# Group statistics of the first layer's output: sums from ScalarE's accumulator output in place of VectorE's bn_stats

## The chip, the cores and the metric

The kernel runs on one core of one Trainium2 chip. The metric is the device time of an execution in microseconds (us), the median of several runs. In what follows PE is the tensor engine (PEld its weight loads), DVE the vector engine, ACT the scalar engine, POOL GpSimd, and SP the engine whose queue issues most of the DMAs.

## The reference

The input `x` is (4, 16, 256, 256) in float32: four images, 16 channels. Two layers follow each other, each with a residual connection:

```python
x = x + _L0_conv_ref(_gn(x), L0_conv_conv_w, L0_conv_conv_b)
x = x + _L1_conv_ref(_gn(x), L1_conv_base_weight, ..., L1_conv_bias_weight)
```

`_gn` normalises each image in 8 groups of two channels: it subtracts the group's mean and divides by sqrt(var + 1e-5), over all 256 x 256 pixels. Layer 0 is a convolution that gives 25 logits for each channel and pixel, a softmax over the 25, and a sum of the 5 x 5 neighbourhood of the normalised `x` weighted by it. Layer 1 is a convolution of SiLU and of eight B-spline bases of its normalised input. What this document is about lies between the two: layer 1's normalisation needs the mean and the variance of each group of layer 0's output `x1`, and an image's statistics are known only once its last pixel is there.

## The kernel before

**Preparation** (to about 142 us). The statistics of `x` are taken with `bn_stats` on DVE, put together over the partitions by a matmul with a matrix of ones (`group_stats`, L132 to L153), and kept for each image as `nrm[b]`: column 0 is the reciprocal standard deviation of each group, column 1 is minus mean times that. So `x * nrm[:, 0] + nrm[:, 1]` is the normalised `x`. Image 0 is normalised here.

**Layer 0** (about 142 to 2110 us) goes over 64 strips: 4 images, 2 halves of 128 rows (the rows lie on the partitions), 8 strips of 32 columns. A strip is eight iterations of four columns. In each iteration:

- PE makes the logits, two columns to a tile `lg`, of which there are three (L775 and L779, two matmuls a column).
- ACT takes their exponential into a tile `e`, of which there are four (two ACTIVATEs of 800 elements, L798).
- POOL multiplies `e` with the neighbourhood `u` into the second half of `e` (L803).
- DVE sums numerator and denominator over the 25 places, for the iteration before (L680). This frees the `e` buffer for the exponential four iterations on.

After a strip's last sums, DVE and ACT make the quotient: `Ln` and `Exp` on ACT (L693, L694), three operations on DVE (L698 to L700), in `seed` and `divide`. POOL subtracts the result from the tile `xc` (`apply`, L706; the signs are such that this adds the layer's output to `x`). `xc` holds 128 columns, so four strips. After the fourth it holds `x1`; its statistics are taken (`statistics`, L711, eight `bn_stats` of 256 elements on DVE, L714) and it is stored to `x1s` by a DMA that ACT issues (`store`, L724).

What is done when is written out by hand: `after(k, f)` puts `f` on a list, and `step()` at the end of each iteration calls what is due. So `f` is emitted behind the work of the (k+1)-th iteration after this one. Each engine works through its instructions in the order in which they were emitted (`in_order`, L571). After the last strip the list is emptied without iterations between.

While an image runs, the next one is normalised (`normalize`, L238) by a generator that is advanced once an iteration: on ACT the normalised rows `hsp` and `ht` (L312, L325) and copies `tt` and `hi` out of PSUM (L340), on PE transposes, on DVE the difference `lo` (L355). For image 3 there is nothing more to normalise. In its place the scales of layer 1 for images 0 and 1 are worked out there (`scales`, L166, advanced twice a strip); those of images 2 and 3 follow in layer 1. `scales` turns the statistics into `q`, whose columns are the scale and the bias with which layer 1 reads `x1`.

**Layer 1** (about 2119 us to the end) has 64 units of 16 rows. Per unit ACT does for each of two halves an `Abs` (L923) and three functions (L158, L159, L160 in `spline`), and one `Silu` (L908). DVE does four operations a half (L161 to L164) and moves the result out of PSUM (L944). PE does 120 matmuls. The instructions of layer 1 that need no more than layer 0's early rows are emitted into the last strips of layer 0: `marks` says behind which instruction of ACT's and SP's queue they may begin. The first `Silu` stands behind the last ACT instruction of layer 0.

Of the kernel before, what the change touches and what calls it, by code (L numbers as in the profile page):

```python
# [11 lines left out]
F32 = mybir.dt.float32  # L12
F32R = mybir.dt.float32r
AF = mybir.ActivationFunctionType
ALU = mybir.AluOpType
AX = mybir.AxisListType
# [17 lines left out]
def conv_preact_kernel(  # L34
# [12 lines left out]
    nc = tc.nc  # L47
    B, C, H, W = x.shape
    G = 8
    GC = C // G  # L50
# [77 lines left out]

    edge = const.tile([P, 5], F32, name="edge")
    stat1 = ctx.enter_context(tc.tile_pool(name="stat1", bufs=1))  # L130
    st1 = [const.tile([P, G, NH * (W // CX), 6], F32, name=f"st1_{b}") for b in range(B)]

    def group_stats(pool, psum, st, name):

# [31 lines left out]
    def scales(b, psum):  # L166


        def small(n, name):
            return stat1.tile([P, n], F32, name=f"{name}_{b}", tag=f"{name}{b % 2}")  # L170

        mv = stat1.tile([P, G, 2], F32, name=f"mv_{b}", tag=f"mv{b % 2}")
        for g in range(G):
            nc.vector.bn_aggr(mv[:, g, :], st1[b][:, g].rearrange("p n s -> p (n s)"))
        yield
        ps = psum()[:, 0:G]
        nc.tensor.matmul(ps, lhsT=ones, rhs=mv[:, :, 0], start=True, stop=True)
        yield
        mean, d, rstd = small(G, "mean"), small(G, "d"), small(G, "rstd")
        q = stat1.tile([P, 6], F32, name=f"q_{b}", tag=f"q{b}")  # L180
        nc.vector.tensor_sub(d, mv[:, :, 0], ps)
        nc.vector.tensor_mul(mean, gsel_sb, ps)
        nc.vector.reduce_sum(q[:, 1:2], mean, AX.X)
        yield
        nc.scalar.activation(d, d, AF.Square)
        yield
        ps = psum()[:, 0:G]
        nc.tensor.matmul(ps, lhsT=ones, rhs=d, start=True, stop=False)
        nc.tensor.matmul(ps, lhsT=ones, rhs=mv[:, :, 1], start=False, stop=True)
        yield  # L190
        nc.vector.tensor_scalar(rstd, ps, EPS, None, ALU.add)  # L191
        yield
        nc.gpsimd.tensor_tensor(rstd, rstd, mhalf, ALU.pow)  # L193
        nc.gpsimd.tensor_mul(rstd, rstd, gsel_sb)
        yield
        nc.vector.reduce_sum(q[:, 0:1], rstd, AX.X)
        nc.vector.tensor_scalar(q[:, 1:2], q[:, 1:2], q[:, 0:1], -1.0, ALU.mult, ALU.mult)
        for k in range(2):
            nc.vector.tensor_scalar(q[:, 2 + k : 3 + k], q[:, k : k + 1], 2.5, None, ALU.mult)
        yield  # L200
        ps = psum()[:, 0:2]
        nc.tensor.matmul(
            ps, lhsT=sel.rearrange("p c s -> p (c s)"), rhs=q[0:C, 2:4], start=True, stop=True
        )
        yield
        nc.vector.tensor_copy(q[:, 4:5], ps[:, 0:1])
        nc.vector.tensor_add(q[:, 5:6], ps[:, 1:2], ub)
        sc[b] = tuple(q[:, k : k + 1] for k in (0, 1, 4, 5))
        yield
# [2 lines left out]


    nrm = [const.tile([P, 2, G], F32, name=f"nrm{b}") for b in range(B)]
    NIM = 3

    def norm_tiles(prep):
# [171 lines left out]
    with tc.tile_pool(name="prep0", bufs=2) as prep, tc.tile_pool(  # L389
# [121 lines left out]
        for b in range(B):  # L511
            st = stat.tile([P, G, NH * (GC if b == 0 else 1), 6], F32, name=f"st0_{b}", tag=f"st0{min(b, 1)}")
            for hf in range(NH):
                n = b * NH + hf
                t = loaded.pop(0)
                for g in range(G):
                    if b == 0:
                        for k in range(GC):
                            nc.vector.bn_stats(st[:, g, hf * GC + k, :], t[:, g * GC + k, :])
                    else:  # L520
                        nc.vector.bn_stats(
                            st[:, g, hf, :],
                            t[:, g * GC : (g + 1) * GC, :].rearrange("p c w -> p (c w)"),
                        )
                    next(ahead, None)
                    next(ahead, None)

                nc.scalar.activation(xq, t, AF.Square)
                sq = pstat.tile([P, W], F32, name=f"sq_{n}", tag="sq")
                for c in range(C):  # L530
                    nc.tensor.matmul(
                        sq, lhsT=idr, rhs=xq[:, c], start=c == 0, stop=c == C - 1
                    )
                nc.vector.tensor_reduce(hm[:, n : n + 1], sq, AX.X, ALU.max)
                next(ahead, None)
                if n >= NH and n + 3 < B * NH:
                    loaded.append(load_x(n + 3))
            mean, rstd = group_stats(stat, pstat, st, f"x{b}")
            nc.vector.tensor_copy(nrm[b][:, 0], rstd)
            nc.vector.scalar_tensor_tensor(nrm[b][:, 1], mean, -1.0, rstd, ALU.mult, ALU.mult)  # L540
            ms = stat.tile([P, 2], F32, name=f"ms_{b}", tag="ms")
            nc.vector.tensor_mul(mean, mean, mean)
            nc.vector.tensor_reduce(ms[:, 0:1], mean, AX.X, ALU.add)
            nc.vector.tensor_scalar(ms[:, 0:1], ms[:, 0:1], 9.0 * GC, None, ALU.mult)
            nc.vector.tensor_reduce(ms[:, 1:2], rstd, AX.X, ALU.max)
            nc.vector.tensor_mul(ms[:, 1:2], ms[:, 1:2], ms[:, 1:2])
            v = hm[:, b * NH : (b + 1) * NH]
            nc.vector.tensor_scalar(v, v, 9.0 / 8.0, ms[:, 0:1], ALU.mult, ALU.add)
            nc.vector.tensor_scalar(v, v, ms[:, 1:2], None, ALU.mult)
            if b == 0:  # L550
                prepare0()
            if b == 1:
                prepare1()
            if b == 0:
                ahead = normalize(0, ptr0, tiles, held, nc.vector.tensor_copy)
                next(ahead)
# [41 lines left out]
    def layer0(shift):  # L598
# [4 lines left out]
        with tc.tile_pool(name=f"prep{arm}", bufs=2) as prep, tc.tile_pool(  # L603
# [64 lines left out]
            def after(k, f, *args):  # L668

                later.append([k, partial(f, *args)])  # L670
# [32 lines left out]
            def apply(n, nd, xc):  # L703
                w0 = strips[n][2] * SW % CX
                v = xc[:, :, w0 : w0 + SW]
                nc.gpsimd.tensor_sub(v, v, nd[:, 1].rearrange("p j c -> p c j"))  # L706
                if w0 + SW == CX:
                    after(2, statistics, n, xc)

            def statistics(n, xc):  # L710
                b, hf, s = strips[n]  # L711
                k = hf * (W // CX) + s * SW // CX
                for g in range(G):
                    nc.vector.bn_stats(  # L714
                        st1[b][:, g, k, :],
                        xc[:, g * GC : (g + 1) * GC, :].rearrange("p c w -> p (c w)"),
                    )
                after(2, store, n, xc)

            def store(n, xc):  # L720
                b, hf, s = strips[n]
# [104 lines left out]
    def layer1(arm, last, marks):  # L826
# [3 lines left out]
        with ExitStack() as pools:  # L830
# [124 lines left out]
            def outputs(n, sx):  # L955
# [27 lines left out]
                waiting.append((b, u, yp))  # L983

            more = chain(*(
                scales(b, lambda: pstat.tile([P, 8], F32, name=f"ps{arm}", tag="ps"))
                for b in range(2, B)
            ))
            for half in range(2):
# [90 lines left out]
```

## Time and profile before

The time is 3223.17 us, the median of three runs (3222.82 to 3223.66). The page of the profiled execution has a span of 3222.0 us:

| engine | busy us | share of the span | instructions |
|---|---|---|---|
| PE | 2862.3 | 89% | 14776 |
| PEld | 1490.7 | 46% | 14776 |
| DVE | 3101.7 | 96% | 1799 |
| ACT | 2208.0 | 69% | 2233 |
| POOL | 1936.4 | 60% | 659 |

These are averages over two stages with different limits. The tenths of the span in 40 slices tell the stages apart: ACT stands at 4 to 6 tenths and POOL at 9 until the 28th slice, and from there ACT at 9 and POOL at 0. DVE stands at 9 nearly throughout.

In the lists of groups, an instruction is named by its line, engine and operation, then by the tiles it writes and reads. "Idle before" is time in which the engine stood still just before these instructions, with what ended it. In lists in order of time the first number is the start, the second the time from the first start to the last end, and "x8" says that eight instructions follow each other.

### The profile page before, as it was taken

Reading aid. Unit: us, or ns where it says so; the run is one execution under the profiler, and the core shown is the slowest. Engines: PE = TensorE matmul, PEld = TensorE weight load, DVE = VectorE, ACT = ScalarE, POOL = GpSimd, SP = SyncE. Lnnn points to the kernel's source line nnn. Section 1 sums busy time; section 2 is a strip of 40 time slices with the busy share of each in tenths; the row PEclk is TensorE's granted clock in tenths of the full one; section 3 lists DMA queues with packets and bytes.
Section 4 is the critical chain, followed back from the end, with each engine's and each line's share of the span. In section 5 each row is a group of like instructions: output and inputs, shape, how many; then the busy total and the mean of one; then the engine's idle time right before and its main releaser. Section 6 shows DMA issues by size and latency. Waiting matters only on the chain. (4 is left out here: it accounts for less than half of the span.)

```text
span 3222.0 us, 40428 instructions
## 1 busy us (share of the span) xinstructions
PE 2862.3 (89%) x14776; PEld 1490.7 (46%) x14776; DVE 3101.7 (96%) x1799; ACT 2208.0 (69%) x2233; POOL 1936.4 (60%) x659
## 2 busy tenths in 40 slices
PE   3499999999999999999999989859999989988988
PEld 3366665666566566656656656512222222222222
DVE  6589999999999999999999999999999999999997
ACT  6366555466554465554444444589999999999996
POOL 2299999999999999999999999900000000000000
PEclk7699999999999999999999999979999999999999
DMA  7988886778877788877756756678878778888883
GB/s 224 291 223 236 229 221 187 212 211 230 246 208 192 203 219 225 249 198 203 210 156 170 191 157 170 163 169 183 178 168 179 180 171 168 180 176 173 178 179 71
DMA packets 356531, 626.34 MB, mean 194 GB/s; under 512 B 45298, under 2 KB 222692, under 8 KB 340452
## 3 DMA queue, kind: packets, MB, share of 16 engines
q1 hardware_dynamic: 323300, 606.88, 75.3%
q10 hardware_dynamic: 33024, 16.78, 1.9%
q8 instruction: 121, 1.98, 0.3%
q14 instruction: 86, 0.70, 0.1%
HBM read 513.95 MB, written 104.24 MB: 192 GB/s over the span
## 5 line engine op out<-in xcount | busy, mean ns | idle before, releaser
L775 PE MATMUL lg<-wm,am 128*128 128x400 f32 x4096 | 1748.9, 508 | 123.4 <-ACT e L798 109.7
L803 POOL TENSOR_TENSOR e<-e,u 128x1600 f32<-128x1600 f32 x512 | 1789.1, 3536 | 68.5 <-ACT e L798 68.0
L680 DVE TENSOR_REDUCE nd<-e 128x128 f32<-128x3200 f32 x512 | 1747.5, 3477 | 23.3 <-POOL e L803 23.2
L798 ACT ACTIVATE e<-lg 128x800 f32<-128x800 f32 x1024 | 815.7, 836 | 896.5 <-DVE nd L680 768.9
L779 PE MATMUL lg<-wn,an 97*128 97x400 f32 x2048 | 1358.4, 663 | 0.5 <-DMA an<-hsl 0.5
L775 PEld LDWEIGHTS lg<-wm,am 128*128 128x128 f32 x4096 | 766.3, 194 | 450.1 <-ACT e L798 161.3
L961 PE MATMUL yp<-ring,wt 128*32 128x512 f32 x6144 | 755.1, 604 | 146.0 <-DVE ring L164 110.4
L779 PEld LDWEIGHTS lg<-wn,an 97*128 97x128 f32 x2048 | 390.8, 191 | 311.9 <-issue 15.6
L961 PEld LDWEIGHTS yp<-ring,wt 128*32 128x32 f32 x6144 | 206.5, 110 | 685.1 <-issue 477.9
L889 POOL MEMSET sx<- 16x256 f32 x8 | 2.4, 303 | 765.6 <-DMA out_dram<-yo 706.6
L977 PE MATMUL yp<-sl,ws 64*32 64x512 f32 x1536 | 176.5, 588 | 0.0
L164 DVE TENSOR_TENSOR ring<-ta,ta 128x2048 f32<-128x2048 f32 (+1 forms) x64 | 147.8, 2309 | 2.5
L164 DVE TENSOR_TENSOR ring<-tb,tb 128x2048 f32<-128x2048 f32 x64 | 145.6, 2276 | 2.6
L163 DVE TENSOR_TENSOR ta<-ta,ta 128x2048 f32<-128x2048 f32 (+1 forms) x64 | 147.3, 2301 | 0.0
L163 DVE TENSOR_TENSOR tb<-tb,tb 128x2048 f32<-128x2048 f32 x64 | 146.5, 2289 | 0.0
L908 ACT ACTIVATE sl<-sx,q 64x2048 f32<-64x2048 f32 x64 | 133.3, 2083 | 0.0
L160 ACT ACTIVATE ta<-ta 128x2048 f32<-128x2048 f32 (+1 forms) x64 | 122.3, 1911 | 0.0
L160 ACT ACTIVATE tb<-tb 128x2048 f32<-128x2048 f32 x64 | 120.5, 1883 | 0.6 <-POOL sx L889 0.6
L193 POOL TENSOR_TENSOR rstd<-rstd,mhalf 128x8 f32<-128x8 f32 x4 | 8.7, 2176 | 175.6 <-DVE rstd L191 175.6
L706 POOL TENSOR_TENSOR xc<-xc,nd 128x512 f32<-128x512 f32 x64 | 98.8, 1544 | 12.1 <-DVE nd L700 12.1
L977 PEld LDWEIGHTS yp<-sl,ws 64*32 64x32 f32 x1536 | 48.8, 106 | 116.2 <-issue 113.2
L923 ACT ACTIVATE xta<-xta,q 128x2048 f32<-128x2048 f32 (+2 forms) x44 | 91.6, 2083 | 0.0
(174 smaller groups left out, 2131.9 us busy)
## 6 DMA issues: line engine op xcount, KB each, us to landing
am<-hst SPq DMA_DIRECT2D x512, 194.6 KB
u<-hs SPq DMA_DIRECT2D x320, 288.0 KB
an<-hsl SPq DMA_DIRECT2D x512, 129.8 KB
xta<-x1s SPq DMA_DIRECT2D x40, 1024.0 KB
xtb<-x1s SPq DMA_DIRECT2D x40, 1024.0 KB
xtc<-x1s SPq DMA_DIRECT2D x40, 1024.0 KB
am<-hst SPq DMA_DIRECT2D x256, 129.8 KB
sx<-x1s SPq DMA_DIRECT2D x248, 128.0 KB
```

Source lines behind the costliest of these rows:

```text
L160: nc.scalar.activation(s1, r1, AF.Square, scale=2.0)
L163: nc.vector.tensor_mul(s1, s1, r1)
L164: nc.vector.tensor_add(f, s2, s1)
L680: nc.vector.tensor_reduce(nd[:, :, j : j + JG, :], e.rearrange("p t j m c d -> p t j c m d"), AX.XY, ALU.add,)
L706: nc.gpsimd.tensor_sub(v, v, nd[:, 1].rearrange("p j c -> p c j"))
L775: nc.tensor.matmul(lg[:, i, :NL], lhsT=am[:, o : o + P], rhs=wm.rearrange("p m c d -> p (m c d)"), start=True, stop=False,)
L779: nc.tensor.matmul(lg[:, i, :NL], lhsT=an[:, o : o + P], rhs=wn.rearrange("p m c d -> p (m c d)"), start=False, stop=True,)
L798: nc.scalar.activation(ev, lg[:, :, :NL], AF.Exp)
L803: nc.gpsimd.tensor_tensor(e[:, 1].rearrange("p j m c d -> p j (m c) d"), e[:, 0].rearrange("p j m c d -> p j (m c) d"), uv, ALU.mult,)
L908: nc.scalar.activation(sl[n % 2][:, :, 1 : W + 1], t, AF.Silu, scale=sc[b][0][0 : RD * C], bias=sc[b][1][0 : RD * C],)
L961: nc.tensor.matmul(yp[t * M : (t + 1) * M], lhsT=wt[:, d, e].rearrange("p r o -> p (r o)"), rhs=ring[:, r0 + t * RT + d : r0 + t * RT + d ...
L977: nc.tensor.matmul(yp[t * M : (t + 1) * M], lhsT=ws[:, e].rearrange("p r o -> p (r o)"), rhs=sl[n % 2][:, t : t + NT + 1 : NT, e : e + W], ...
```

## The change

`bn_stats` and `bn_aggr` leave layer 1's statistics. In their place each group of `xc` is passed twice over ACT, once as `Identity` and once as `Square`, both with scale `nrm[b][:, 0]` and bias `nrm[b][:, 1]` of the group of `x`. So ACT forms z = (x1 - mean of x) / std of x, and its accumulator output gives the sum of z and of its square over the 256 elements; the written tile `z` itself is read by nobody. The sums of z and of z squared give mean and variance of x1 in units of the group of `x`, which keeps both near the size of one. The purpose is to take the statistics off DVE, which is the busiest engine in layer 0.

The statistics are also spread: one group in each of eight iterations instead of all eight at once, from one iteration earlier on. The store of `xc` is no longer put off behind the statistics and comes three iterations earlier, behind the second group. `scales` is rewritten for the sums: fewer operations on DVE, one matmul instead of three, and five operations on POOL instead of two. It needs `nrz[b]`, two more small operations an image in the preparation.

```diff
--- before
+++ after
@@ -128,7 +128,10 @@
-    st1 = [const.tile([P, G, NH * (W // CX), 6], F32, name=f"st1_{b}") for b in range(B)]
+    NK = NH * W // CX
+    st1 = [const.tile([P, 2, G, NK], F32, name=f"st1_{b}") for b in range(B)]
@@ -169,32 +172,29 @@ scales
-        mv = stat1.tile([P, G, 2], F32, name=f"mv_{b}", tag=f"mv{b % 2}")
-        for g in range(G):
-            nc.vector.bn_aggr(mv[:, g, :], st1[b][:, g].rearrange("p n s -> p (n s)"))
+        sums, d, mz, p = small(2 * G, "sums"), small(G, "d"), small(G, "mz"), small(G, "p")
+        q = stat1.tile([P, 6], F32, name=f"q_{b}", tag=f"q{b}")
+        nc.vector.tensor_reduce(sums, st1[b].rearrange("p t g k -> p (t g) k"), AX.X, ALU.add)
         yield
-        ps = psum()[:, 0:G]
-        nc.tensor.matmul(ps, lhsT=ones, rhs=mv[:, :, 0], start=True, stop=True)
+        ps = psum()[:, 0 : 2 * G]
+        nc.tensor.matmul(ps, lhsT=ones, rhs=sums, start=True, stop=True)
         yield
-        mean, d, rstd = small(G, "mean"), small(G, "d"), small(G, "rstd")
-        q = stat1.tile([P, 6], F32, name=f"q_{b}", tag=f"q{b}")
-        nc.vector.tensor_sub(d, mv[:, :, 0], ps)
-        nc.vector.tensor_mul(mean, gsel_sb, ps)
-        nc.vector.reduce_sum(q[:, 1:2], mean, AX.X)
+        part = 1.0 / (GC * CX * NK)
+        nc.scalar.activation(d, ps[:, 0:G], AF.Square, scale=part)
         yield
-        nc.scalar.activation(d, d, AF.Square)
+
+        nc.vector.scalar_tensor_tensor(mz, ps[:, 0:G], part, nrm[b][:, 1], ALU.mult, ALU.subtract)
+        nc.vector.scalar_tensor_tensor(d, ps[:, G : 2 * G], part, d, ALU.mult, ALU.subtract)
         yield
-        ps = psum()[:, 0:G]
-        nc.tensor.matmul(ps, lhsT=ones, rhs=d, start=True, stop=False)
-        nc.tensor.matmul(ps, lhsT=ones, rhs=mv[:, :, 1], start=False, stop=True)
+        nc.gpsimd.tensor_add(d, d, nrz[b][:, 1])
+        nc.gpsimd.tensor_tensor(p, d, mhalf, ALU.pow)
+        nc.gpsimd.tensor_mul(d, p, nrz[b][:, 0])
+        nc.gpsimd.tensor_mul(p, p, gsel_sb)
+        nc.gpsimd.tensor_mul(p, p, mz)
         yield
-        nc.vector.tensor_scalar(rstd, ps, EPS, None, ALU.add)
-        yield
-        nc.gpsimd.tensor_tensor(rstd, rstd, mhalf, ALU.pow)
-        nc.gpsimd.tensor_mul(rstd, rstd, gsel_sb)
-        yield
-        nc.vector.reduce_sum(q[:, 0:1], rstd, AX.X)
-        nc.vector.tensor_scalar(q[:, 1:2], q[:, 1:2], q[:, 0:1], -1.0, ALU.mult, ALU.mult)
+        nc.vector.reduce_sum(q[:, 0:1], d, AX.X)
+        nc.vector.reduce_sum(q[:, 1:2], p, AX.X)
+        nc.vector.tensor_scalar(q[:, 1:2], q[:, 1:2], -1.0, None, ALU.mult)
...
+    nrz = [const.tile([P, 2, G], F32, name=f"nrz{b}") for b in range(B)]
@@ -538,6 +541,8 @@
             nc.vector.scalar_tensor_tensor(nrm[b][:, 1], mean, -1.0, rstd, ALU.mult, ALU.mult)
+            nc.gpsimd.tensor_mul(nrz[b][:, 0], rstd, gsel_sb)
+            nc.vector.scalar_tensor_tensor(nrz[b][:, 1], rstd, EPS, rstd, ALU.mult, ALU.mult)
@@ -705,17 +710,20 @@ apply, statistics
                 if w0 + SW == CX:
-                    after(2, statistics, n, xc)
-
-            def statistics(n, xc):
+                    for g in range(G):
+                        after(1 + g, statistics, n, xc, g)
+                    after(2, store, n, xc)
+
+            def statistics(n, xc, g):
                 b, hf, s = strips[n]
                 k = hf * (W // CX) + s * SW // CX
-                for g in range(G):
-                    nc.vector.bn_stats(
-                        st1[b][:, g, k, :],
-                        xc[:, g * GC : (g + 1) * GC, :].rearrange("p c w -> p (c w)"),
-                    )
-                after(2, store, n, xc)
+                z = l0.tile([P, GC * CX], F32, name=f"z_{n}_{g}{arm}", tag="z")
+                v = xc[:, g * GC : (g + 1) * GC, :].rearrange("p c w -> p (c w)")
+                for t, f in enumerate((AF.Identity, AF.Square)):
+                    nc.scalar.activation(
+                        z, v, f, scale=nrm[b][:, 0, g : g + 1], bias=nrm[b][:, 1, g : g + 1],
+                        accum_out=st1[b][:, t, g, k : k + 1],
+                    )
```

More of the change, by code (lines that the diff above doesn't have):

```diff
@@ L985, in layer1 @@
             more = chain(*(
-                scales(b, lambda: pstat.tile([P, 8], F32, name=f"ps{arm}", tag="ps"))
+                scales(b, lambda: pstat.tile([P, 2 * G], F32, name=f"ps{arm}", tag="ps"))
                 for b in range(2, B)
```

## The prediction

> **What bounds the kernel now.** I read the busy time by stretch first, then groups, waits, and single engines in order of time. Layer 0 with image 1 to 3's normalisation runs from about 171 to 2110 us, layer 1 from 2119.5 on. The busy time in these stretches (length, then PE, weight loads, DVE, ACT, POOL, each with its count):
>
> ```profile
> 171.00:2110.00 1939.00, 1810.90 (x6297) 1169.58 (x6295) 1928.05 (x906) 1043.87 (x1532) 1872.66 (x577) 0.98 0.75 203
> 2110.00:2119.50 9.50, 0.00 (x0) 0.00 (x0) 9.21 (x12) 3.25 (x4) 1.38 (x9) 0.50 0.85 209
> 2119.50:3222.00 1102.50, 981.77 (x8208) 267.40 (x8208) 1059.40 (x609) 1072.05 (x570) 22.49 (x27) 0.98 0.80 169
> ```
>
> In layer 0 DVE is busy 99.4%, POOL 96.6%, ACT 54%. In layer 1 ACT works without a gap until 3195 us (its waits after 2119.5 are none). So the change takes work from the engine that bounds layer 0 and gives it to the engine that bounds layer 1, but mostly while that one idles. The groups (line, engine, operation, tiles, shapes, count, busy us, mean ns, idle before):
>
> ```profile
> L680 DVE TENSOR_REDUCE nd<-e 128x128 f32<-128x3200 f32 x512 | 1747.5, 3477 | 23.3 <-POOL e L803 23.2
> ...
> L798 ACT ACTIVATE e<-lg 128x800 f32<-128x800 f32 x1024 | 815.7, 836 | 896.5 <-DVE nd L680 768.9 <-PE lg L779 109.7 <-DVE q L196 3.7
> L714 DVE BATCH_NORM_STATS2 st<-xc 128x6 f32<-128x256 f32 x128 | 43.2, 410 | 1.6 <-POOL xc L706 1.6
> ```
>
> ACT's exp waits for DVE's reduce to free one of the four `e` buffers. The other waits of layer 0, in the list of who waited for whom between 171 and 2110 us:
>
> ```profile
> ACT e L798 <- PE lg L779: 95.0, 138, 2.8
> POOL e L803 <- ACT e L798: 54.0, 46, 3.6
> DVE nd L680 <- POOL e L803: 15.1, 4, 13.4
> ```
>
> DVE waited for POOL 15 us in all (13.4 at the start): the ring exp, multiply, reduce, free buffer is paced by DVE. What one strip costs DVE stands in its order of time:
>
> ```profile
> 1032.47 0.68 DVE L355 TENSOR_TENSOR lo<-tp,hi 128x512 fp32r<-128x512 f32 x1
> 1033.07 27.23 DVE L680 TENSOR_REDUCE nd<-e 128x128 f32<-128x3200 f32 x8
> 1060.22 2.70 DVE L714 BATCH_NORM_STATS2 st<-xc 128x6 f32<-128x256 f32 x8
> 1062.84 0.67 DVE L698 TENSOR_TENSOR nd<-nd,r 128x512 f32<-128x512 f32 x1
> ...
> 1064.88 27.23 DVE L680 TENSOR_REDUCE nd<-e 128x128 f32<-128x3200 f32 x8
> 1092.02 0.68 DVE L698 TENSOR_TENSOR nd<-nd,r 128x512 f32<-128x512 f32 x1
> ```
>
> From start to start: eight reduces 27.15, the division (three operations) 2.04, a `lo` 0.60, the statistics 2.62. A strip is 29.19, with a `lo` 29.79, and with statistics 2.62 longer. POOL's strip:
>
> ```profile
> 2048.30 27.91 POOL L803 TENSOR_TENSOR e<-e,u 128x1600 f32<-128x1600 f32 x8
> 2076.14 1.56 POOL L706 TENSOR_TENSOR xc<-xc,nd 128x512 f32<-128x512 f32 x1
> 2077.64 17.47 POOL L803 TENSOR_TENSOR e<-e,u 128x1600 f32<-128x1600 f32 x5
> ```
>
> 27.84 for eight multiplications and 1.50 for the subtraction: 29.34. That is the next bound. PE starts one logits column every 0.855 us: 32 columns are 27.4, about 28 with the transposes.
>
> **What the Trainium skill says.** "ScalarE: Activation LUTs", What ACT_TABLE_LOAD costs: an ACTIVATE takes 186 + 0.833 N ns, and 93 ns more for each per-partition pointer operand. The trace agrees: L923 (scale and bias pointers, N = 2048) reads 2083 ns against 2078. "SBUF — State Buffer", Who interferes with whom: a DVE instruction with one SBUF input outside the 2-port modes does not contend with GpSimd. The multiplication reads 3505 to 3592 ns over the whole of layer 0, so nothing in the trace contradicts it, and removing bn_stats will not speed POOL. No row shows ScalarE's accumulator output. The nearest statement is on VectorE ("VectorE: DVE Perf Modes", Two Vector instructions with no wait between them): there an operation that writes out its accumulator is two instructions. I use it only to put an upper end on the cost.
>
> **The change part by part.**
>
> Removed from DVE: 128 bn_stats in 16 bursts of eight. One burst (2110.23) falls in the tail behind the last reduce, so 15 count. Images 0 to 2 contain twelve: DVE needs 29.79 on most strips afterwards, POOL 29.34, PE 28, so DVE stays the bound and all is gained: 12 x 2.62 = 31.4 us.
>
> Image 3 has no `lo`. DVE before: 16 x 29.19 + 3 x 2.62 + some 5.2 for the small operations of two `scales` = 480.1. After: 16 x 29.19 + 3.2 = 470.2, as bn_aggr (8 x 0.14 in a row) and a few more go. POOL: 16 x 29.34 + 5.4 (two powers of 1.69, eight small operations of about 0.2 to 0.25) = 474.8. POOL takes over here: 5.3 is gained, or up to 9.9 if its lead at the start carries it. A lead of one multiplication (3.5) is what I take, less a little: 8.5 us.
>
> Added to ACT: 256 ACTIVATEs of N = 256. From L923: 2083 - 0.833 x 1792 = 590 ns; the second of a pair waits for the first, which costs a gap of 35 ns as between L693 and L694. The accumulator read costs between nothing and about 0.2 (the shortest ACT rows, 8-element copies, are 194 ns): I take 0.1. A pair is 1.45 (1.25 to 1.65), eight 11.6 (10.0 to 13.2).
>
> In layer 0 one pair stands behind the two exps of each of eight iterations. An iteration is 3.4 to 3.7 us; exps 1.57 and a pair 1.45 are 3.0. Beside them lie Ln and Exp (1.2 a strip) and normalisation: its ACT groups sum to 201 us over 48 strips, 4.2 each, 5.4 where it is dense. A strip with statistics then needs 12.6 + 11.6 + 1.2 + 0.4 for the store's issue + 5.4 = 31.2 of ACT against 29.8: late by 1.4 at its end. And the first Identity waits for POOL's subtraction, with the next exps queued behind it. Let DVE end reduce S-2 at T. As DVE never waits after POOL's subtraction today, POOL ends multiplication S by about T+1.9, the subtraction by T+3.4. Exps S+2 run to T+1.6, the pair T+3.4 to 4.9, exps S+3 to T+6.5. POOL does S+1 and S+2, whose input is there, until T+10.4. So exps may be some 4 us late before POOL starves, and 1.4 + 1.8 fits. In the likeliest case all of it is hidden.
>
> The way into layer 1 is not hidden. Today:
>
> ```profile
> 2108.15 1.89 ACT L159 ACTIVATE tb<-xta 128x2048 f32<-128x2048 f32 x1
> 2110.22 0.37 ACTq L724 DMA_DIRECT2D x1s<-xc  x1
> 2110.64 1.91 ACT L160 ACTIVATE tb<-tb 128x2048 f32<-128x2048 f32 x1 [0.59 <-POOL sx L889]
> 2118.20 1.28 ACT L908 ACT_TABLE_LOAD   x1 [5.65 <-DMA x1s<-xc]
> 2119.49 2.10 ACT L908 ACTIVATE sl<-sx,q 64x2048 f32<-64x2048 f32 x1
> ```
>
> The last subtraction ends at 2110.2; the store lands 8 us later, and the first silu starts 9.3 after the subtraction. In the changed order the last sixteen ACTIVATEs, with the store after the first four, stand ahead of L158 to L160 of `tb`. These three used ACT's idle time before; now all follow the subtraction: 11.6 + 0.4 + 5.5 + 1.3 = 18.8, against 9.3. The store lands at 2.9 + 8 = 10.9, before that. ACT has no slack in layer 1 (17.06 us a unit, back to back, where DVE waits 0.3), so the end moves by 9.5 us (7.9 to 11.1). DVE's 2.7 us of statistics there are gained for nothing.
>
> The rest: `nrz` (two small operations an image, 0.2 each, beside DMA waits) up to 0.5. `scales` of images 2 and 3 in layer 1 spares DVE about 1 us each where ACT is the bound: 0. The earlier store: 0, since no layer-1 load of these rows waits until the end.
>
> Sum: 3223.2 - 31.4 - 8.5 + 9.5 + 0.5 = 3193.
>
> **The rivals.**
>
> A, POOL's idle time stays. POOL waits 54 us for exps in layer 0, 0.84 a strip. If later exps keep that, a strip cannot go under 30.2, on average against 30.44 now: images 0 to 3 gain about 16 us, and with the transition the time is 3217. For it: ACT is late more often. Against it: those waits appear because POOL has run ahead to the end of the buffers.
>
> B, ACT's queue costs part. If half the statistics strips (dense normalisation) lose 2 us, the gain falls by some 16: 3209. PE has only 1.8 us a strip to make up what a blocked exp costs it.
>
> C, slower. With an accumulator read of 0.4 a pair is 2.05. A dense strip needs 12.6 + 16.4 + 1.2 + 0.4 + 5.4 + 1.8 (wait) = 37.8 on ACT, against 32.4 now: 8 x 5.4 lost there, 7 x 2.62 gained elsewhere, transition 14: 3223 + 43 - 18 + 14 = 3262. If only the transition and a third of this come, about 3232. Against it: no ACT row is that dear.
>
> **How the numbers follow.** Likeliest 0.68, B 0.14, A 0.08, C 0.10. The time is 3193. Down: the full 9.9 in image 3, 7.9 at the transition, no coupling give 3190, and some more if POOL needs less, 3184. Up to B's 3209, a little over for A: 3212. Faster by over 0.2% (under 3216.7): the likeliest, B and half of A, 0.87; within 0.2% 0.04; slower 0.09.
>
> **What would show it.** DVE strips with a `lo` at 29.8 and none at 32.4; in image 3 strips of about 29.3 with DVE waiting for POOL; a z pair near 1.45 and ACT at some 63% in layer 0; silu 18 to 20 us after the last subtraction; layer 1 unchanged in length after it. Wrong: DVE's reduce waiting for POOL and POOL for exps in the strips with statistics, or PE waiting on exps far above today's 99 us.

## The result and the profile after

The changed kernel takes 3201.5 us in the median (3198.9 to 3205.0), the kernel before, run beside it, 3223.0. The ratio is 0.9934 (95% interval 0.9917 to 0.9951). It is faster by 21.5 us, inside the predicted range and on the side that was predicted, but 8.5 us short of the predicted 3193.

The profiled executions have spans of 3222.0 and 3200.4 us. I cut both at the same events: the start of the first strip's division, of image 3's first division, of the last division, and of the first `Silu` of layer 1. The lines have moved: the division is L703 to L705 now, the reduce L685, the exp L806, the multiplication L811, the subtraction L711, `z` L723, the spline's functions on ACT L161 to L163, the `Silu` L916.

| stretch | before, us | after, us | difference | predicted |
|---|---|---|---|---|
| start to the first division | 208.6 | 207.9 | -0.7 | +0.5 |
| images 0 to 2 (48 strips) | 1462.7 | 1433.8 | -28.9 | -31.4 |
| image 3 (to the last division) | 435.2 | 430.9 | -4.3 | -8.5 |
| last division to the first `Silu` | 13.0 | 22.3 | +9.2 | +9.5 |
| first `Silu` to the end | 1102.5 | 1105.5 | +3.0 | 0 |

The whole of the shortfall is in three rows: 2.5 us in images 0 to 2, 4.2 in image 3, 3.0 after the first `Silu`; the other two rows give 1.5 back. The border between the first two of these is not the prediction's. The last interval of images 0 to 2 already holds the first operations of image 3's two `scales` (`bn_aggr` before, a reduce now), where DVE gained 1.7 us that the prediction counts with image 3. Counted its way, images 0 to 2 gained 27.2 us of 31.4, and image 3 gained 6.0 of 8.5.

The busy time by stretch of the changed kernel (length, then PE, weight loads, DVE, ACT, POOL, each with its count; then the granted clock, the DMA share, GB/s):

```profile
171.00:2077.00 1906.00, 1801.49 (x6287) 1158.96 (x6285) 1889.81 (x772) 1185.93 (x2009) 1872.31 (x583) 0.99 0.78 206
2077.00:2095.00 18.00, 0.00 (x0) 0.00 (x0) 11.16 (x5) 17.25 (x37) 6.00 (x9) 0.50 0.54 132
2095.00:3200.00 1105.00, 975.12 (x8200) 267.36 (x8200) 1052.66 (x591) 1072.06 (x570) 30.31 (x33) 0.98 0.80 169
```

In layer 0 ACT went from 54% to 62%, and DVE is still the busiest at 99.2%, with POOL at 98.2%. The middle stretch has doubled, from 9.5 to 18 us, and ACT fills it: 37 instructions, 17.25 us.

The groups of the changed kernel that answer to those of before:

```profile
L806 ACT ACTIVATE e<-lg 128x800 f32<-128x800 f32 x1024 | 816.4, 837 | 705.2 <-DVE nd L685 505.4 <-PE lg L787 186.2 <-PE lg L783 4.0
...
L723 ACT ACTIVATE z<-xc,nrm 128x256 f32<-128x256 f32 x256 | 153.6, 600 | 17.9 <-POOL xc L711 13.5
...
L723 ACT ACTIVATION_READ_ACCUMULATOR z<-xc,nrm 128x1 f32 x256 | 49.1, 192 | 0.0
```

The accumulator output is an instruction of its own, 192 ns, and the ACTIVATE has 600 ns. ACT idles 705 us ahead of the exps, not 897: the new work went into that idle time.

Who waited for whom in layer 0 (171 to 2080 us):

```profile
DVE nd L685 <- POOL e L811: 20.8, 11, 12.5
...
POOL e L811 <- ACT e L806: 15.8, 14, 3.8
```

POOL waits less for exps than before (15.8 us, 54.0 before), though ACT has more to do. DVE waits for POOL 20.8 us, 5.7 more than before; 12.5 of it is the start of the layer, 3.6 falls in image 3 (0.9 before). So in images 0 to 2 the ring is still paced by DVE.

In image 3 it is POOL that works without a gap. POOL from image 3's first division to the end of its last subtraction but one (length, POOL busy, clock, DMA share, GB/s), first before the change, then after it:

```profile
1671.30:2096.50 425.20, 416.51 (x132) 0.98 0.65 168
...
1641.70:2065.50 423.80, 423.17 (x139) 0.99 0.67 170
```

It stood idle for 8.7 us there before, and for 0.6 us now.

A strip on DVE, in order of time, at the place where `bn_stats` used to stand:

```profile
1045.62 0.70 DVE L704 SCALAR_TENSOR_TENSOR r<-nd,r 128x512 f32<-128x512 f32 x1
1046.36 0.69 DVE L705 TENSOR_TENSOR nd<-nd,r 128x512 f32<-128x512 f32 x1
1046.96 27.23 DVE L685 TENSOR_REDUCE nd<-e 128x128 f32<-128x3200 f32 x8
1074.11 0.68 DVE L703 TENSOR_TENSOR nd<-nd,r 128x512 f32<-128x512 f32 x1
```

The eight reduces are followed at once by the next division. (A "strip" here, and in what follows, is the time from one division to the next.) Most strips of images 0 to 2 with a `lo` take 29.79 us from division to division, and the strips with statistics are like the rest; they took 32.41 before.

### The profile page after: what moved, and what is told of

Read it like the earlier page. It is cut to its first block, busy times and chain, and to the rows that moved or that the text cites. A ratio compares the mean times of both kernels' runs of the same rounds, so it can differ in the third digit from the quotient of the medians.

```text
span 3200.4 us, 40766 instructions
## 1 busy us (share of the span) xinstructions
PE 2847.0 (89%) x14760; PEld 1480.5 (46%) x14760; DVE 3060.2 (96%) x1643; ACT 2364.5 (74%) x2745; POOL 1950.5 (61%) x675
## 4 chain that ended last, share of the span: by engine, by line
DVE 51%; ACT 23%; issue 10%; DMA 6%; PE 5%; POOL 3%; SPq 2%; ACTq 0%; POOLq 0%; DVEq 0%
DVE nd L685 42%; ACT sl L916 3%; ACT ta L161 3%; PE lg L783 3%; ACT tb L163 3%; ACT tb L161 3%; POOL e L811 3%; ACT ta L163 3%; ACT xta L931 2%; ACT xtc L931 2%; ACT xtb L931 2%; DMA xin<-in_x_dram 2%; DVE r L704 1%; DMA an<-hsl 1%; DVE ta L165 1%
## 5 line engine op out<-in xcount | busy, mean ns | idle before, releaser
L811 POOL TENSOR_TENSOR e<-e,u 128x1600 f32<-128x1600 f32 x512 | 1789.7, 3565 | 37.5 <-ACT e L806 29.0
L685 DVE TENSOR_REDUCE nd<-e 128x128 f32<-128x3200 f32 x512 | 1749.3, 3477 | 29.3 <-POOL e L811 29.1
L787 PE MATMUL lg<-wn,an 97*128 97x400 f32 x2048 | 1346.0, 657 | 13.5 <-DMA an<-hsl 13.3
L806 ACT ACTIVATE e<-lg 128x800 f32<-128x800 f32 x1024 | 816.4, 837 | 705.2 <-DVE nd L685 505.4
L723 ACT ACTIVATE z<-xc,nrm 128x256 f32<-128x256 f32 x256 | 153.6, 600 | 17.9 <-POOL xc L711 13.5
L916 ACT ACTIVATE sl<-sx,q 64x2048 f32<-64x2048 f32 x64 | 133.4, 2084 | 2.8 <-DMA sx<-x1s 2.8
L163 ACT ACTIVATE ta<-ta 128x2048 f32<-128x2048 f32 (+1 forms) x64 | 122.4, 1912 | 0.0
L163 ACT ACTIVATE tb<-tb 128x2048 f32<-128x2048 f32 x64 | 120.5, 1883 | 0.0
L711 POOL TENSOR_TENSOR xc<-xc,nd 128x512 f32<-128x512 f32 x64 | 101.8, 1591 | 9.2 <-DVE nd L705 9.2
```

The costliest lines, as they stand in the source:

```text
L163: nc.scalar.activation(s1, r1, AF.Square, scale=2.0)
L685: nc.vector.tensor_reduce(nd[:, :, j : j + JG, :], e.rearrange("p t j m c d -> p t j c m d"), AX.XY, ALU.add,)
L787: nc.tensor.matmul(lg[:, i, :NL], lhsT=an[:, o : o + P], rhs=wn.rearrange("p m c d -> p (m c d)"), start=False, stop=True,)
L806: nc.scalar.activation(ev, lg[:, :, :NL], AF.Exp)
L811: nc.gpsimd.tensor_tensor(e[:, 1].rearrange("p j m c d -> p j (m c) d"), e[:, 0].rearrange("p j m c d -> p j (m c) d"), uv, ALU.mult,)
L916: nc.scalar.activation(sl[n % 2][:, :, 1 : W + 1], t, AF.Silu, scale=sc[b][0][0 : RD * C], bias=sc[b][1][0 : RD * C],)
```

## The experiments

After the result I had three theories: (1) the +9.2 us on the way into layer 1 is the last sixteen `z` ACTIVATEs standing ahead of the spline's functions, (2) the loss in images 0 to 2 comes from the earlier store, which makes SP's queue stand longer and the logits' inputs come late, (3) image 3 is paced by POOL, and there the five POOL operations of `scales` show in full. Their common rival is ACT's queue: the `z` pairs hold up the exps behind them, and what is lost in layer 0 is theirs. Diffs are against the changed kernel unless said otherwise.

### The transition: the last burst back on DVE

```diff
-                    for g in range(G):
-                        after(1 + g, statistics, n, xc, g)
+                    if n // 4 >= len(strips) // 4 - 1:
+                        after(2, statistics_dve, n, xc)
+                    else:
+                        for g in range(G):
+                            after(1 + g, statistics, n, xc, g)
```

`statistics_dve` is eight `bn_stats` into a tile of their own; `scales` of image 3, in layer 1, turns them into the two sums.

> The changed kernel, but the last four strips of image 3 give their statistics by bn_stats on DVE; bn_aggr and the conversion to sums of z follow in layer 1's scales. Theory 1 (the transition costs because sixteen ACTIVATEs stand ahead of layer 1's first functions on ACT, the engine that bounds layer 1, and because the store behind four of them lands late): the first silu starts 9 to 10 us after the last subtraction instead of 17.5, the second 17.1 after the first instead of 20.0; the time is 3201.5 - 8 - 3 = about 3190. Rival (layer 1's end is set by DVE, so what ACT lost there was hidden): 2.7 us go back to DVE and the time stays at 3200 to 3204.

Measured: 3188.0 us (3186.5 to 3191.9), ratio 0.9888 (0.9873 to 0.9903), 13 us under the changed kernel. ACT in order of time, first in the changed kernel, where the train of the last sixteen `z` ACTIVATEs begins and where it ends:

```profile
2077.43 0.60 ACT L723 ACTIVATE z<-xc,nrm 128x256 f32<-128x256 f32 x1 [4.85 <-POOL xc L711]
2077.93 0.18 ACT L723 ACTIVATION_READ_ACCUMULATOR z<-xc,nrm 128x1 f32 x1
2078.15 0.60 ACT L723 ACTIVATE z<-xc,nrm 128x256 f32<-128x256 f32 x1
...
2088.04 1.91 ACT L161 ACTIVATE tb<-xta 128x2048 f32<-128x2048 f32 x1
...
2094.87 2.09 ACT L916 ACTIVATE sl<-sx,q 64x2048 f32<-64x2048 f32 x1
```

and in this experiment:

```profile
2075.99 1.90 ACT L163 ACTIVATE tb<-xta 128x2048 f32<-128x2048 f32 x1
...
2087.27 2.09 ACT L941 ACTIVATE sl<-sx,q 64x2048 f32<-64x2048 f32 x1
```

From 2077.43 to 2088.04 ACT does nothing but `z`; only then come the three functions of `tb`, the table load and the `Silu`, 17.5 us after the end of the last subtraction. With the burst on DVE two of the functions run before the subtraction is done (it ends at 2078.02) and the `Silu` starts 9.25 us after it, as in the kernel before. The second `Silu` follows 17.07 us later, not 20.0, so the +3.0 of the last row of the table goes too. Theory 1 holds: the trace gains 9.3 us between the last division and the first `Silu` (12.98, against 22.26) and 2.7 after it. The subtraction is also shorter here (1.52 us, against 2.57), but that is worth nothing: in the next experiment, without a train, it takes 2.57 again and the `Silu` comes 12.99 us after the last division. With the train its claim on memory goes too; the last experiment tells the two apart.

### No statistics at all

The eight `after(1 + g, statistics, ...)` are taken out, and `st1` is filled with constants.

> The changed kernel without any statistics of x1: the ACTIVATEs that give z are left out and constants stand in their place, so layer 1's scales are not those of the data. The store is early as in the changed kernel. Theory 2 with POOL as image 3's bound: the last reduce ends at about 2068, hardly before 2069.5, since the z pairs cost layer 0 almost nothing; only the transition is gained, and the time is about 3189. Rival (ACT's queue costs part of layer 0's gain): the last reduce ends at 2063 or earlier, and the time is 3183 or less.

Measured: 3186.9 us (3183.8 to 3188.5), 0.9885 (0.9869 to 0.9900). Image 3 takes 430.79 us, against 430.89 with `z`; images 0 to 2 together 1430.9, against 1433.8. So 240 of the 256 ACTIVATEs, with all their pairs and waits, cost layer 0 at most 3 us, and nothing in image 3: there the common rival falls. The strip at the head of image 1 is long here too (31.00 us, instead of 29.79), so it does not take `z` to delay it. What is left of the transition is 8.2 us from subtraction to `Silu`, and 17.07 to the second. This kernel is 14.6 us under the changed one, of which the transition with what follows is the larger part.

### All eight groups at once

```diff
-                        after(1 + g, statistics, n, xc, g)
+                        after(2, statistics, n, xc, g)
```

> The changed kernel with the eight pairs of a statistics strip in one iteration (16 ACTIVATEs, some 10.5 us of ACT in a row) instead of one pair in each of eight. Theory (exps may be about 4 us late before POOL starves, so one pair of 1.3 us an iteration hides and ten microseconds do not): DVE stalls 3 to 5 us in each of 15 bursts; the time is 3246 to 3282. Rival (ACT is busy only 63% of layer 0, so the order of its work does not matter): the time stays under 3210.

Measured: 3266.6 us (two runs), 1.0133 (1.0114 to 1.0151), slower than the kernel before. Who waited for whom in its layer 0 (171 to 2140 us):

```profile
ACT e L806 <- PE lg L787: 450.5, 491, 3.9
...
POOL e L811 <- ACT e L806: 81.8, 40, 6.5
DVE nd L685 <- POOL e L811: 73.2, 60, 12.2
```

A train of 8 x 1.31 = 10.5 us in front of the exps lengthens the strip by 3.6 to 5.7 us in fourteen of the fifteen cases. The other 5 to 7 us are swallowed by the ring's four buffers, somewhat more than the "some 4 us" of slack that the prediction worked out. POOL then waits for exps for 6.5 us at the longest. PE, which had been stopped by the full logits tiles, cannot catch up at once: ACT waits for it 450 us, against 170. So the spreading over eight iterations is what makes the change pay. The DVE work removed is the same here. (The store, too, stands behind the whole train.)

### The spreading and the earlier store without ACT

The kernel before, with only its `bn_stats` spread over the iterations and the store put where the change has it:

```diff
-                    after(2, statistics, n, xc)
+                    for g in range(G):
+                        after(1 + g, statistics, n, xc, g)
+                    after(2, store, n, xc)
```

> The kernel before with the schedule of the change alone: bn_stats stays on DVE, but one group in each of eight iterations, and the store comes three iterations earlier. Theory (DVE bounds layer 0, so moving its work in time gains nothing): 3223 to 3225, every statistics strip still 2.6 us longer. Rival (the gain comes from taking the burst of eight apart): 3210 or less. Theory 2 adds: if the early store costs layer 0 some 2 us by late loads, the time is 3225 to 3227 and PE waits for am here too.

Measured: 3221.75 us, 0.9997 (0.9989 to 1.0006): no difference. The gain comes from DVE's work leaving, not from its new places. Nor does the earlier store cost the kernel before anything, although PE waits 12.7 us for the logits' inputs `am` here, which it did not before.

### The store three iterations later

```diff
-                    after(2, store, n, xc)
+                    after(2 if n == len(strips) - 1 else 5, store, n, xc)
```

> The changed kernel with the store of xc put off by three more iterations, to where it was before, except for the very last store. Theory 2 (part of layer 0's missing gain comes from the earlier store: SP's queue, which fetches ahead, stands 11 to 15 us behind it at the loads of u, and the loads of am and an behind these come late): SP's waits for the store fall from 166 us in layer 0 to 120 or less, PE no longer waits for am (18 us in the changed kernel), the last reduce ends at about 2067 instead of 2069.5, the time is about 3199 and its spread is smaller. Rival (the z pairs on ACT delay the exps by themselves): the strips that lost 1 to 2 us still lose them, 3201 to 3202.

Measured: 3204.4 us (3198.6 to 3204.9), 0.9938 (0.9924 to 0.9951): no gain in time. The trace says something else than the time. In the changed kernel three strips behind a store are long (30.75, 30.89 and 32.38 us, at the heads of images 1 and 2 and in the middle of image 2, instead of 29.79, 29.79 and 30.39). At the head of image 1 the way can be followed: SP's queue stands 11.0 us for a store, then PE waits 4.8 us for `am`, POOL 3.8 us for the exps behind it, and DVE 0.8 us for POOL. In layer 0 as a whole SP's queue, which issues the loads of the logits' inputs, stands 166 us for stores (10.6 to 13 us at a time on average), against 122 before. Here those three strips are at their usual length, SP stands 140 us where 120 or less was expected, and the last reduce ends 3.3 us earlier. But PE still waits 14.1 us for `am` (18.2 in the changed kernel), another strip is long (30.81 us, near the end of image 0), and this trace is of the fastest of the five runs, and three of the others are near 3204. So the place of the loss and the late loads are seen, that the store's place is their cause is not shown, and theory 2 is not confirmed.

### The changed kernel once more

> The changed kernel once more, as the measure for the runs beside it and for the spread of its time. All theories: 3201 to 3204; the transition as before (first silu 17.5 us after the last subtraction, second 20.0 after the first). In layer 0 the strips that lost time: theory 2 (the early store holds SP's queue) says the same ones, at the head of an image and around SP's waits of 11 us or more; the rival (chance meetings of transfers) says other strips than in the first trace.

Measured: 3199.95 us (3198.1 to 3203.5), 0.9932 (0.9918 to 0.9945). Image 3 takes 430.78 us (430.89 in the first profile), the second `Silu` follows 20.04 us after the first again. The lost strips are those at the heads of images 1 and 2 once more (31.13 and 30.29), but not the third. The three images differ from the first profile by 2.3 us in sum: what is lost there varies from execution to execution, the other two losses do not.

### The POOL operations of `scales` on DVE and ACT

For images 0 and 1:

```diff
-        nc.gpsimd.tensor_add(d, d, nrz[b][:, 1])
-        nc.gpsimd.tensor_tensor(p, d, mhalf, ALU.pow)
-        nc.gpsimd.tensor_mul(d, p, nrz[b][:, 0])
...
+            nc.vector.tensor_add(d, d, nrz[b][:, 1])
+            nc.scalar.activation(p, d, AF.Ln)
+            nc.scalar.activation(p, p, AF.Exp, scale=-0.5)
+            yield
+            nc.vector.tensor_mul(d, p, nrz[b][:, 0])
```

> The changed kernel with the five POOL operations of the scales of images 0 and 1 (2.8 us each time, in image 3 of layer 0) given to DVE (four, 0.15 us each) and ACT (the power as Ln and Exp, 0.2 us each). Theory 3 (POOL bounds image 3: a strip is 29.34 there, and the two strips of 31.3 and 32.5 us are long because of these operations): image 3 shortens by 4 to 5 us, the two long strips become 29.3 to 30, the time is 3197 to 3199. Rival (DVE still bounds image 3, or the long strips come from waits on ACT and PE within scales): image 3 stays or grows by 1 us, 3201 to 3204.

Measured: 3214.9 us, 0.9976 (0.9968 to 0.9984), 15 us slower than the changed kernel beside it and a clear miss. All engines of this kernel in order of time:

```profile
1740.61 0.16 DVE L190 TENSOR_TENSOR d<-d,nrz 128x8 f32<-128x8 f32 x1
...
1740.80 0.21 ACT L191 ACTIVATE p<-d 128x8 f32<-128x8 f32 x1 [10.68 <-DVE d L190]
...
1742.78 3.52 POOL L820 TENSOR_TENSOR e<-e,u 128x1600 f32<-128x1600 f32 x1 [4.68 <-ACT e L815]
```

The addition stood on DVE behind three reduces. The `Ln` that needs it came up on ACT 10.68 us earlier and held the exps queued behind it, until POOL had nothing left for 4.68 us. That strip became 33.73 us long, against 31.29. The next one, 42.35 us against 32.50, has another cause. DVE in order of time, three of the six small multiplications:

```profile
1778.31 0.17 DVE L195 TENSOR_TENSOR p<-p,gsel_sb 128x8 f32<-128x8 f32 x1
...
1794.23 3.44 DVE L195 TENSOR_TENSOR p<-p,gsel_sb 128x8 f32<-128x8 f32 x1
1797.70 3.44 DVE L196 TENSOR_TENSOR p<-p,mz 128x8 f32<-128x8 f32 x1
```

The six, which I had counted with 0.15 us each, took 3.55, 0.17, 0.17, 2.02, 3.44 and 3.44 us, 12.8 in all, and stood on DVE, which paces the reduces. Together the two strips are 12.3 us longer, nearly all of the 12.7 that image 3 lost. So the queue cost some 2.4 us, and the length of the small operations the rest. Seven of the nine whole strips behind took 29.19 to 29.20 us, DVE's pace and not POOL's 29.34. But in the 42.35 us POOL had begun ten multiplications, not eight, and so was ahead; this says nothing on theory 3.

The same edit together with the last burst on DVE:

> Both corrections together: the last statistics on DVE as in e1_tail_dve, and the scales of images 0 and 1 off POOL as in e7_scales_dve. They lie in different places, so the theories add them: 3188 - 4 = 3184 (3182 to 3187). If POOL does not bound image 3: 3188 to 3190.

Measured: 3201.35 us (3199.9 to 3204.9), 0.9932 (0.9919 to 0.9946), with the same two long strips (33.72 and 44.07 us), where 3184 was expected. It is 13.5 us under the edit alone: the transition's gain adds to it in full.

### `scales` of image 1 in layer 1

```diff
-                        first_scales = [scales(k, partial(lambda k: bank[:, k], k)) for k in range(2)]
+                        first_scales = [scales(0, lambda: bank[:, 0]), iter(())]
...
-                for b in range(2, B)
+                for b in range(1, B)
```

> The changed kernel, with the scales of image 1 worked out in layer 1 (where POOL idles and they are due at unit 16) and only those of image 0 in image 3 of layer 0. Nothing is given to ACT or to DVE, and no wait stands in front of an exp that did not before. Theory 3 (POOL bounds image 3, so the five small POOL operations, 2.8 us, cost their length): one of the two long strips (31.2 and 32.5 us) becomes 29.2 to 29.4 and the fifteen intervals of image 3 sum to 428 instead of 430.8; the time falls by 2 to 3, to 3197 to 3198. Rival (POOL is hidden there): 430 to 431 and no change of the time.

Measured: 3197.8 us (3194.3 to 3198.4), 0.9918 (0.9905 to 0.9932), and image 3 takes 428.5 us instead of 430.9. This is the test of theory 3. POOL of the changed kernel in order of time, where `scales` of image 0 passes:

```profile
1739.17 0.29 POOL L189 TENSOR_TENSOR d<-d,nrz 128x8 f32<-128x8 f32 x1
1739.54 1.64 POOL L190 TENSOR_TENSOR p<-d,mhalf 128x8 f32<-128x8 f32 x1
...
1741.98 7.03 POOL L811 TENSOR_TENSOR e<-e,u 128x1600 f32<-128x1600 f32 x2
```

The five operations hold POOL from 1739.17 to 1741.98, 2.8 us, and the strips of the two `scales` are 31.29 and 32.50 us long. With one of them gone there is one long strip (31.6) and image 3 is 2.4 us shorter. POOL's own sum, 14 strips x 29.34 + 15.5 for the last interval + 2 x 2.8, is 431.9 us, and with one `scales` 429.1; measured are 430.9 and 428.5. DVE's, with 29.19 a strip and the 1.5 us that its small operations for both `scales` measure in these intervals (0.75 with one), is 425.7 and 424.9. Image 3 follows POOL in both kernels, with a lead of 0.6 to 1.0 us and not one of a multiplication. The gain says so too: DVE was spared 0.75 us here and POOL 2.8, and image 3 gained 2.4. Theory 3 holds.

### The last burst on DVE, and `scales` of image 1 in layer 1

The two edits that helped, together.

> e1_tail_dve and e9_scales1_late in one kernel: the last statistics on DVE, the scales of image 1 in layer 1. Theories 1 and 3 add: 3188 - 2.5 = about 3185.5 (3183 to 3188). If POOL does not bound image 3: 3188 to 3190. Here too nothing of the computation is left out.

Measured: 3185.4 us (3183.2 to 3188.9), 0.9884 (0.9869 to 0.9899). Image 3 takes 428.2 us, the `Silu` starts 9.1 us after the last subtraction ends, the second 17.07 later. This version beats both kernels: 37.7 us under the one before, 16.1 under the changed one. It is about what no statistics in layer 0 at all would give.

### The store ahead of the last `z`

```diff
                 if w0 + SW == CX:
+                    if n == len(strips) - 1:
+                        after(1, store, n, xc)
...
-                    after(2, store, n, xc)
+                    if n < len(strips) - 1:
+                        after(2, store, n, xc)
```

> The changed kernel, with only the very last store put ahead of the last sixteen ACTIVATEs instead of behind the first four. Theory 1, taken apart: the first silu stays at 17.5 us after the last subtraction (the ACTIVATEs still stand ahead of it), but the store lands 2 us earlier and the second silu no longer waits for the load of sx: 17.1 after the first instead of 20.0. The time is 3200 - 3 = about 3197. Rival (the late second silu has another cause): 20.0 stays, 3200 to 3203.

Measured: 3202.5 us (3199.6 to 3204.7), 0.9934 (0.9920 to 0.9947). The second `Silu` still follows 20.15 us after the first, with 2.98 us of waiting for `sx`. So it is not the last store that delays it; my explanation of the +3.0 fell.

### `z` in memory of its own

```diff
+    zt = [const.tile([P, GC * CX], F32, name=f"zt{k}") for k in range(2)]
...
-                z = l0.tile([P, GC * CX], F32, name=f"z_{n}_{g}{arm}", tag="z")
+                z = zt[g % 2]
```

> The changed kernel with the tiles z in memory of their own instead of in layer 0's pool. In e11_store_first the second silu came 20.1 us after the first as before, so the store is not what delays it; in the trace the load of xtb stands 18.5 us for an ACTIVATE that writes z, and the loads of xtc and sx stand behind it on SP's queue. Theory (layer 1's tile xtb takes over memory of z, so its load waits for the last of the sixteen ACTIVATEs): xtb's load starts right after the last reduce, about 8 us before the first z, sx arrives in time, the second silu starts 17.1 us after the first, and the time falls by 3, to about 3197 to 3199. The first silu stays at 17 to 17.5 us after the last subtraction. Rival (sx is late for another cause): 20.0 stays, 3200 to 3203.

Measured: 3195.9 us (3190.9 to 3197.7), 0.9911 (0.9898 to 0.9925), 5.6 us under the changed kernel. SP's queue in order of time, in the changed kernel:

```profile
2088.04 1.16 SPq L887 DMA_DIRECT2D xtb<-x1s  x2
2089.31 1.20 SPq L887 DMA_DIRECT2D xtc<-x1s  x2
2090.55 2.02 SPq L901 DMA_DIRECT2D sx<-x1s  x4
```

and with `z` in its own tiles:

```profile
2071.77 1.16 SPq L888 DMA_DIRECT2D xtb<-x1s  x2
```

In the changed kernel the load of layer 1's `xtb` waits 18.5 us for the last `z`, which is what SP's waits name (`SPq L887` for `ACT z L723`): `xtb` lies where `z` lay in layer 0. It goes out at 2088.04, in the instant at which the train of `z` ends, and with it four transfers (two each of `xtb` and `xtc`, 1 MB each in the list of DMAs) run ahead of the second unit's `sx`. With `z` elsewhere two of the four go out right after the last reduce, 18.6 us earlier when both are measured from the last division, and the second `Silu` follows after 17.09 us. That settles the +3.0. Nor is `xtb` alone in this: in the changed kernel the first writes of layer 1's `ring` wait for `z` as well (5.6 us on DVE, 8.1 on POOL), though nothing of `ring` reads `z`; here they do not. The first `Silu` I had expected at 17 to 17.5 us after the subtraction; it came after 13.7. Two functions of `tb` now run ahead of the `z` train, beside POOL's subtraction, which I had not foreseen. So the reuse of the memory was also one reason for the functions standing behind `z`, not the order of the queues alone.

## Why the prediction was right, and where it was wrong

**What bounds layer 0.** Right. DVE paced it and still does; removing 2.62 us from a statistics strip shortened that strip by 2.62 (32.41 to 29.79), and the spread `bn_stats` in the kernel before, with the same DVE work, gained nothing.

**ACT's new work is hidden in layer 0.** Right, and it is the largest claim. A pair steps by 1.31 us, where 1.45 (1.25 to 1.65) was taken: the ACTIVATE was estimated well (590 ns, measured 600 in the mean), and the read of the accumulator takes not 0.1 but 0.19. It begins some 0.1 before its ACTIVATE ends, though, and the store's issue takes ACT no time. Taking all `z` away gives layer 0 at most 3 us, and nothing in image 3. Rival A (POOL's idle time stays) is refuted by POOL's waits, 15.8 us instead of 54.0; rivals B and C by the strips with statistics, which are as long as the others. (Rival A's present average of 30.44 us a strip does not come out of the trace: the 62 whole strips average 30.36.) The burst shows that B and C had a real mechanism: without the spreading it costs 3.6 to 5.7 us a strip, and the kernel is slower than before.

**Images 0 to 2.** The step "all is gained" was nearly right: 27.2 us of 31.4. All twelve bursts are gone, and three strips at heads and in the middle of images lost 4.2. (The table's 28.9 has 1.7 more, which are DVE's operations of `scales`.) I had costed the earlier store at nothing, since no load of layer 1 needs it. But SP's queue, which also carries the loads of the logits' inputs, stands longer for stores now. Whether this is the cause stays open: the late store removes those three losses from its trace and not from its time.

**Image 3.** Right in mechanism, wrong in one term. "A lead of one multiplication (3.5) is what I take, less a little: 8.5 us." The lead was worth 1 us at most. POOL takes over, as the step itself says, with 29.34 us strips and the five operations of each `scales` in full; DVE waits for it 3.6 us there, and 6.0 us were gained (4.3 in the table, and the 1.7 above), near the lower end that the step gave (5.3). DVE's small operations of both `scales`, put at 5.2 us before and 3.2 after, measure 4.0 and 1.8. Why POOL brings no greater lead into image 3 was not tested. Moving one `scales` out of image 3 gave 2.4 us back.

**The transition.** Right in mechanism and size: +9.2 for +9.5. The terms differ, though, and cancel. The `Silu` comes 17.5 us after the subtraction, not 18.8, since the train is 10.6 us (11.6) and the store's 0.4 lies beside it. The subtraction itself takes 2.57 us, not 1.52, where a multiplication on DVE now runs beside it. The order of the queues was taken as the cause; the last experiment shows that the memory of `z` is part of it, as without that claim the `Silu` comes 3.8 us earlier.

**After the first `Silu`.** The step "The rest: ... 0" failed. I checked which rows the loads of layer 1 need and not which memory they go to. `z` is read by nobody, but it occupies memory that layer 1 loads into, so its last writer became something that a DMA waits for: 3.0 us.

**Preparation.** +0.5 was expected, -0.7 measured. In the traces of the changed kernel and its variants this stretch takes 206.1 to 209.4 us, so neither number can be told from noise.

Together: 4.2 + 2.5 + 3.0 of shortfall, less 1.2 in the preparation and 0.3 at the transition, are the 8.2 us between the two spans' difference and the predicted one.

## What to carry to other kernels

Work that leaves the bounding engine pays only up to the next engine's pace, so compare the two strip by strip: here 0.45 us a strip lay between DVE and POOL in one part of the layer, and in the other part the order was reversed. Look separately at the last instance of repeated work, where the engine that had been idle becomes the one that everything waits for; a mixed version, with the last burst left on the old engine, was worth 13 us. And ask of every new tile, even one that nobody reads, what will be loaded into its memory next, and of every new small instruction what is queued behind it while it waits, and what runs beside it.

## What the runs showed of the hardware

- ScalarE's accumulator output has an instruction of its own in the trace: 185 to 236 ns, 192 in the mean, after each ACTIVATE. An ACTIVATE of 256 elements with two pointers and its read step by 0.59 to 0.72 us in a row.
- Tiny VectorE operations can be very long beside GpSimd. The 128 x 8 additions and multiplications with two inputs in SBUF, moved to DVE in the seventh experiment, took 0.16 to 0.17 us where POOL stood idle. Beside POOL's multiplications of 3.5 us they took 3.55 us once, and 2.02, 3.44 and 3.44 us in a row, each ending about when one of these did. This agrees with the Trainium skill, "SBUF — State Buffer", Who interferes with whom, which says that a DVE instruction with two SBUF inputs contends with a GpSimd instruction that reads SBUF. The reduce with its one input keeps its 3.48 us beside the same multiplications.
- The same shows at the layer change: POOL's subtraction takes 2.57 us and DVE's multiplication 3.75 where they overlap; where they don't, in the first experiment, they take 1.52 and 2.56.
